# Four places instead of two for raw weight chunks in a fused four-layer kernel

## The chip, the cores and the metric

One core of one Trainium2 chip runs the whole program. Its engines are named as in the profile: PE does matrix products (PEld is its weight load), DVE, ACT and POOL work element by element, and the queue of SP (SPq in the profile) issues nearly all DMAs. The metric is the device time of one launch in microseconds. Of the kernel before, three runs were timed: 2829.66, 2829.91 and 2830.13 us, median 2829.91 us.

## What is computed

The input `x` has 16 batches of 256 positions by 256 features. Four layers are applied, each added to its own input:

- Layer 0: a gated running average along the positions, with 16 decays of its own, their blend, two gates, a product and a layer norm.
- Layer 1: per batch a softmax over masked scores, and the average that it weights.
- Layer 2: eight experts and a shared one, each `silu(h Wg) * (h Wu)` and then `Wd`, with 1024 hidden features. All nine are applied to every batch and summed with weights of the batch. In the kernel they are nine experts, so the weights of layer 2 are read as 9 x 8 = 72 chunks of 128 hidden features.
- Layer 3: `gelu(h W1 + b1)`, then `W2` for 192 of the features and one of eight small matrices, chosen by batch, for the other 64.

```
x = x + _L0_cond_ref(x, ...)
x = x + _L1_cond_ref(x, L1_cond_W1, L1_cond_b1, L1_cond_v, itok_B_0_2)
x = x + _L2_cond_ref(x, fside_Bx8_0, condB_sharedgateprob[:, None], ...)
x = x + _L3_cond_ref(x, itok_B_0_7, ...)
```

## The kernel before

**Numbers in two parts.** Every matrix product of layers 2 and 3, and those of layers 0 and 1 from batch 1 on, is made of three passes (`mm3`, L101 to L103). Each operand is split into a rounded high part (`rnd`, L88, on ACT) and the rest (`low`, L95, on DVE or POOL), and high x high, high x low and low x high are added up.

**Side work and unit work.** Layers 0 and 1 of a batch are two generators, `traces(b)` (21 steps) and `pooled(b)` (10 steps); here they are called side work. Batch 0 has versions of its own, `first_traces` and `first_pooled`. The last step of `pooled(b)` adds the result to `acc` (L460) and calls `split_x2` (the rows x<-acc), which writes the two parts of layer 2's input. Layer 2 is done by `l2_unit`, one unit for one chunk of two batches, or for two chunks of one batch: products into `pg` and `pu`, the SiLU on ACT (L742), `h` on DVE (L743), its two parts `hh` (L88 on ACT, L95 on POOL), and, two units later, the product into `y`. Each unit works on 512 columns in all.

**Order of the units.** A list called `plan` goes through positions; position p applies expert p mod 9. Batch 0 alone takes positions 0 to 4, batches 0 and 1 take 5 to 8, batch 1 alone 9 and 10. From position 11 on the next pair rides as well, so that each chunk is used by two groups; layer 3 of the first pair comes after position 13. A unit for both batches of a pair needs `pooled` of both to be done. Between units the loop calls `step()`, which advances the side work at a pace worked out from due times; in program order `pooled(1)` ends at the 16th of the 20 units of batch 0 alone. From then on what a step issues on DVE and PE is put behind the `h` and the product last issued in program order. A planner in the framework then orders each engine's instructions by priority and by its own estimate of times. Loads of chunks are given a priority 400 places ahead (`BOOST`).

**The weight chunks.** `load_chunk` brings a chunk (128 x 768 numbers, 384 KB) into a raw tile by a DMA on SP's queue (L672). ACT writes its high part and DVE or POOL its low part into a tile of the ring `w` (L88 and L95, rows w_e<-raw_e). A raw tile can be loaded anew when both have read it. The ring has ten places (`RING`); a place is free when the last product of its chunk is done. The raw tiles have two places (the pool `raws`). From position 11 on, both parts of a chunk are also written out to memory (`keep`, L696), and from position 20 on chunks come from there, without raw tiles (L665). So 160 chunks go through raw tiles: 88 of positions 0 to 10 and 72 of positions 11 to 19. In positions 0 to 4, POOL makes the low part of every third chunk or so, and DVE the others.

**The tiles of the pairs' inputs.** Layer 2's and layer 3's inputs of a pair (`x2`, `x3`) lie in the pool `xs`, which has three places of 128 x 2048 numbers. At the start one of them holds small weights (`raw_a`, in the profile small_a). The inputs of pairs 0 and 1 take two of them (first written at 59.9 and 339.7 us), and the next tile wanted is that of the first pair's layer 3, first written at 523.9 us.

Of the kernel before, what the change touches and what calls it, by code (L numbers as in the profile page):

```python
# [8 lines left out]
F32 = mybir.dt.float32  # L9
# [9 lines left out]
P = 128  # L19
# [6 lines left out]
SLACK = 16  # L26
L0_BUFS = {"bt": 3, "tr": 3, "mod": 2, "hA": 2, "hB": 2}
SECOND = 11
APART = 5
LAG = 2  # L30
BOOST = 400
# [13 lines left out]
def fused_kernel(  # L45
# [27 lines left out]
    raws = ctx.enter_context(tc.tile_pool(name="raws", bufs=2))  # L73
    xs = ctx.enter_context(tc.tile_pool(name="xs", bufs=3))
# [11 lines left out]
    def rnd(e, out_, in_):  # L86
        if e == "a":
            last_of["ca"] = A.activation(out_, in_, AF.Copy)  # L88
        elif e == "v":
            V.tensor_copy(out_, in_)  # L90
        else:
            G.tensor_scalar(out_, in_, 1.0, 1.0, ALU.mult, ALU.mult)

    def low(e, out_, in_, h):
        i = (V if e == "v" else G).tensor_tensor(out_, in_, h.bitcast(F32), ALU.subtract)  # L95
        if e == "v":
            last_of["cv"] = i
        return i
# [557 lines left out]

    kept = {}

    def load_chunk(key):
        kind = key[0]  # L660
        again = (kind, key[2])
        if kind != "c" and again in kept:
            t = ring.tile([P, 2, 768], F32R, tag="w", name="w_" + "_".join(map(str, key[:2])) + f"_{key[-1]}")
            n = 768 if kind == "e" else 384
            nc.sync.dma_start(t.bitcast(F32)[:, :, :n], kept[again])  # L665
            ring_tiles[key] = t
            return
        raw = raws.tile([P, 768], F32, tag="raw", name="raw_" + "_".join(map(str, key)))
        t = ring.tile([P, 2, 768], F32R, tag="w", name="w_" + "_".join(map(str, key[:2])) + f"_{key[-1]}")
        if kind == "e":  # L670
            n = 768
            nc.sync.dma_start(raw, wexp[key[2]])  # L672
        elif kind == "f":
            n = 384
            nc.sync.dma_start(raw[:, :n], w3[key[2]])
        else:
            n = 512
            b, i = key[1], key[2]
            nc.sync.dma_start(
                raw[:, :520],  # L680
                comb[bass.ds(eregs[b], 1), i].rearrange("o p c -> (o p) c"),
            )
            if i == 0:
                V.tensor_copy(bias3[:, b : b + 1], raw[:, 512:513])
        rnd("a", t[:, 0, :n], raw[:, :n])
        e = "v"
        if kind == "e" and key[1] == 0:

            e = "g" if key[2] < 2 else "v" if key[2] < 6 else "gv"[key[2] % 2]
        elif kind == "e" and key[1] < ALONE and key[2] % 3 == 0:  # L690
            e = "g"
        low(e, t[:, 1, :n], raw[:, :n], t[:, 0, :n])
        ring_tiles[key] = t
        if kind == "e" and key[1] >= SECOND or kind == "f":
            d = keep.tile([P, 2, n], F32, name="keep_" + "_".join(map(str, again)))
            nc.sync.dma_start(d, t.bitcast(F32)[:, :, :n])  # L696
            kept[again] = d
# [145 lines left out]
    for k in range(1, NB // 2):  # L843
        p0 = SECOND + NX * ((k - 1) // 2) + (0 if k % 2 else APART)
        rides.append((p0, p0 + NX, (2 * k, 2 * k + 1)))
# [4 lines left out]
    for pos in range(max(r[1] for r in rides)):  # L850
        e = pos % NX
# [24 lines left out]
    def prefetch(n, boost=BOOST):  # L876
        while n > 0 and nxt[0] < len(order):
            k = order[nxt[0]]
            if k[0] == "c" and k[1] not in eregs:
                eregs[k[1]] = nc.sync.value_load(eix[0:1, k[1] : k[1] + 1], min_val=0, max_val=NE - 1)  # L880
            with tc.high_priority(offset=boost) if boost else nullcontext():
                load_chunk(k)
            nxt[0] += 1
            n -= 1
# [102 lines left out]
    for i, item in enumerate(plan):  # L987
        kind, args, _, done = item[:4]
# [130 lines left out]
```

## Time and profile before

| what | value |
|---|---|
| median of three runs | 2829.91 us |
| the profiled execution, its time | 2829.02 us |
| its span, first to last instruction | 2827.0 us |
| mean granted clock of PE | 0.996 |
| PE, DVE, ACT, POOL busy | 2774.3, 1454.9, 1248.6, 1299.3 us |
| loads of expert chunks into raw tiles | 160, of 384 KB, 11.7 to 859.0 us, median 3.7 us to landing |
| read and written by DMA | 310.91 MB read, 64.21 MB written |

Times of views are microseconds from the start of the span. A line of the waits reads "who waited, for whom: total us, times, longest us". A line of the windows reads "stretch, its length, then for PE, PEld, DVE, ACT and POOL busy us and instructions, then PE's granted clock, the busy share of the DMA engines, and GB/s". A line of a tile's view reads "line, engine, operation, out<-in, count: shortest/median/longest ns, first and last start".

### The profile page before, as it was taken

How to read it: one execution, taken by the hardware profiler on the slowest of the kernel's cores; microseconds unless marked ns; L12 is line 12 of the kernel's file. 1: busy time of each engine (PE TensorE's matmuls, PEld its weight loads, DVE VectorE, ACT ScalarE, POOL GpSimd, SP SyncE). 2: the span in 40 equal slices, each digit the busy share in tenths (PEclk: the TensorE clock that was granted, in tenths of full speed). 3: DMA queues.
4: the chain of work that ended last, by engine and by line, in shares of the span. 5: the costliest groups of instructions: out<-in, count | busy, mean ns of one | idle time of the engine just before them, and what ended most of it. 6: DMA issues, size and time to landing. Idle time of an engine off the chain costs nothing.

```text
span 2827.0 us, 36929 instructions
## 1 busy us (share of the span) xinstructions
PE 2774.3 (98%) x13604; PEld 2331.4 (82%) x13604; DVE 1454.9 (51%) x2662; ACT 1248.6 (44%) x2062; POOL 1299.3 (46%) x986
## 2 busy tenths in 40 slices
PE   7889999999999999999999999999999999999999
PEld 4877898888888888888888888888888888888888
DVE  6988877865666363544545444444444542222222
ACT  5565565465444533435334443344433453233334
POOL 5755645544545353544534444444444443333333
PEclk9999999999999999999999999999999999999999
DMA  4453376396443533324433153331533242222453
GB/s 118 138 153 118 104 242 214 121 309 207 151 150 123 177 114 105 120 81 135 153 107 106 41 179 112 108 120 62 177 101 112 92 162 98 90 90 89 167 177 118
DMA packets 116998, 377.53 MB, mean 134 GB/s; under 512 B 12898, under 2 KB 31186, under 8 KB 116818
## 3 DMA queue, kind: packets, MB, share of 16 engines
q1 hardware_dynamic: 116386, 375.11, 40.1%
q8 instruction: 108, 1.77, 0.3%
q14 instruction: 72, 0.59, 0.1%
q10 hardware_dynamic: 432, 0.06, 0.0%
HBM read 310.91 MB, written 64.21 MB: 133 GB/s over the span
## 4 chain that ended last, share of the span: by engine, by line
PE 82%; DVE 7%; DMA 4%; ACT 3%; issue 2%; POOL 1%; SPq 0%; DVEq 0%; ACTq 0%; POOLq 0%
PE pg L102 8%; PE pg L103 8%; PE pg L101 8%; PE pu L103 8%; PE pu L102 8%; PE pu L101 8%; PE y L103 8%; PE y L102 8%; PE y L101 8%; DMA raw_e<-in_wexp_dram 4%; DVE w_e L95 2%; DVE tr L331 1%; ACT w_e L88 1%; PE z L101 1%; PE z L103 1%
## 5 line engine op out<-in xcount | busy, mean ns | idle before, releaser
L95 POOL TENSOR_TENSOR hh<-h,hh 128x512 fp32r<-128x512 f32 x640 | 847.7, 1325 | 1318.8 <-ACT hh L88 1298.2
L743 DVE TENSOR_TENSOR h<-h,pu 128x512 f32<-128x512 f32 x576 | 393.9, 684 | 907.4 <-PE pu L103 805.6
L88 ACT ACTIVATE hh<-h 128x512 fp32r<-128x512 f32 x640 | 403.5, 631 | 933.8 <-DVE h L743 911.6
L101 PE MATMUL pg<-x,w_e 128*128 128x512 f32 (+1 forms) x1232 | 466.0, 378 | 10.2 <-DVE h L743 6.4
L742 ACT ACTIVATE h<-pg 128x512 f32<-128x512 f32 x576 | 343.1, 596 | 299.1 <-PE pg L103 236.5
L101 PE MATMUL pu<-x,w_e 128*128 128x512 f32 (+1 forms) x1232 | 465.3, 378 | 6.9 <-ACT h L742 6.7
L103 PE MATMUL pg<-x,w_e 128*128 128x512 f32 (+1 forms) x1232 | 464.6, 377 | 1.5 <-DVE w_e L95 1.2
L102 PE MATMUL pg<-x,w_e 128*128 128x512 f32 (+1 forms) x1232 | 464.4, 377 | 1.1 <-POOL x L95 1.1
L102 PE MATMUL y<-hh,w_e 128*128 128x512 f32 (+1 forms) x1232 | 462.8, 376 | 2.2 <-POOL hh L95 2.2
L102 PE MATMUL pu<-x,w_e 128*128 128x512 f32 (+1 forms) x1232 | 463.5, 376 | 0.0
L103 PE MATMUL pu<-x,w_e 128*128 128x512 f32 (+1 forms) x1232 | 463.4, 376 | 0.0
L103 PE MATMUL y<-hh,w_e 128*128 128x512 f32 (+1 forms) x1232 | 462.7, 376 | 0.0
L101 PE MATMUL y<-hh,w_e 128*128 128x512 f32 (+1 forms) x1232 | 416.2, 377 | 2.8 <-ACT hh L88 1.6
L335 POOL TENSOR_TENSOR ta<-ta,tr 128x512 f32<-128x512 f32 x225 | 310.5, 1380 | 87.3 <-DVE tr L331 77.1
L331 DVE TENSOR_TENSOR_SCAN tr<-decay,bt 128x256 f32<-128x256 f32 x450 | 285.6, 671 | 0.0
L101 PEld LDWEIGHTS pg<-x,w_e 128*128 128x128 f32 x1232 | 232.3, 189 | 54.1 <-DVE h L743 8.9
L101 PEld LDWEIGHTS pu<-x,w_e 128*128 128x128 f32 x1232 | 232.5, 189 | 50.4 <-ACT h L742 9.5
L101 PEld LDWEIGHTS y<-hh,w_e 128*128 128x128 f32 x1232 | 231.5, 189 | 46.8 <-ACT hh L88 2.6
L102 PEld LDWEIGHTS y<-hh,w_e 128*128 128x128 f32 x1232 | 232.4, 189 | 44.6 <-POOL hh L95 2.9
L103 PEld LDWEIGHTS pg<-x,w_e 128*128 128x128 f32 x1232 | 232.4, 189 | 44.4 <-DVE w_e L95 2.0
L103 PEld LDWEIGHTS pu<-x,w_e 128*128 128x128 f32 x1232 | 232.5, 189 | 41.9
L103 PEld LDWEIGHTS y<-hh,w_e 128*128 128x128 f32 x1232 | 232.3, 189 | 41.8
(279 smaller groups left out, 3263.2 us busy)
## 6 DMA issues: line engine op xcount, KB each, us to landing
w_e<-keep_e SPq DMA_DIRECT2D x216, 768.0 KB, 4.2
raw_e<-in_wexp_dram SPq DMA_DIRECT2D x160, 384.0 KB, 3.7
keep_e<-w_e SPq DMA_DIRECT2D x72, 768.0 KB, 4.3
mod<-mdd SPq DMA_DIRECT2D x120, 256.0 KB, 3.6
w_f<-keep_f SPq DMA_DIRECT2D x56, 384.0 KB, 3.5
raw_c<-in_comb_dram SPq DMA_DIRECT2D x32, 260.0 KB, 2.7
xr<-in_xT_dram SPq DMA_DIRECT2D x16, 256.0 KB, 3.5
xt<-in_x_dram SPq DMA_DIRECT2D x16, 256.0 KB, 2.6
```

The source lines that it names most:

```text
L88: last_of["ca"] = A.activation(out_, in_, AF.Copy)
L95: i = (V if e == "v" else G).tensor_tensor(out_, in_, h.bitcast(F32), ALU.subtract)
L101: PE.matmul(o, wh, xh, start=start, stop=False, **kw)
L102: PE.matmul(o, wh, xl, start=False, stop=False, **kw)
L103: last_of["pe"] = PE.matmul(o, wl, xh, start=False, stop=stop, **kw)
L331: V.tensor_tensor_scan(tr[:, c], decay[:, d : d + 1].to_broadcast([P, S]), bt[:, c], 0.0, ALU.mult, ALU.add)
L335: G.tensor_tensor(tacc, tacc, tr, ALU.add)
L742: A.activation(h, ps_g, AF.Silu)
L743: last_of["h"] = V.tensor_tensor(h, h, ps_u, ALU.mult)
```

## The change

One more tile, `spare`, is taken from the pool `xs`, so that it is the second of its three places; it is a whole tile of 2048 numbers per partition, of which two stretches of 768 are used, at 0 and at 1024. Chunks are counted as they are loaded, and of every four, two go to the pool `raws` as before and two into the halves of `spare`, as long as they are chunks of positions 0 to 11 (96 chunks). All other chunks go to `raws`, whose two places remain. Nothing else is changed: not the ring, not the loads or their sizes, not the order in which the program asks for them.

```
+SPARE = 12
...
+    spare = xs.tile([P, 2048], F32, tag="x2", name="spare")
+    n_raw = [0]
+
+    def raw_place(key):
+        n_raw[0] += 1
+        if key[0] == "e" and key[1] < SPARE and n_raw[0] % 4 > 1:
+            o = (n_raw[0] % 4 - 2) * 1024
+            return spare[:, o : o + 768]
+        return raws.tile([P, 768], F32, tag="raw", name="raw_" + "_".join(map(str, key)))
...
-        raw = raws.tile([P, 768], F32, tag="raw", name="raw_" + "_".join(map(str, key)))
+        raw = raw_place(key)
```

## The prediction

> **What bounds the kernel now.** I read the page first: PE is busy for nearly the whole span, and its idle time lies in the first eighth.
>
> ```profile
> PE 2774.3 (98%) x13604; PEld 2331.4 (82%) x13604; DVE 1454.9 (51%) x2662; ACT 1248.6 (44%) x2062; POOL 1299.3 (46%) x986
> ...
> PE   7889999999999999999999999999999999999999
> ```
>
> PE idles for 2827.0 - 2774.3 = 52.7 us. Whatever the change does, it can't win more than that, apart from clock. The second view is a table by stretches, cut where batch 0's units begin (60), where both batches' units begin (188.4), and at 345 and 408, about where chunks of the later positions begin.
>
> ```profile
> 0.00:60.00 60.00, 44.71 (x124) 23.07 (x124) 43.00 (x104) 33.45 (x72) 35.31 (x36) 0.89 0.42 117
> ...
> 60.00:80.00 20.00, 19.85 (x162) 19.39 (x162) 15.19 (x28) 12.83 (x20) 9.98 (x7) 1.00 0.41 133
> 80.00:120.00 40.00, 32.27 (x243) 29.63 (x242) 38.03 (x68) 18.08 (x27) 34.30 (x23) 1.00 0.46 142
> 120.00:188.40 68.40, 58.48 (x443) 56.33 (x443) 49.61 (x79) 44.55 (x73) 37.97 (x26) 0.95 0.49 148
> 188.40:345.00 156.60, 148.31 (x690) 120.46 (x691) 139.71 (x230) 85.67 (x140) 95.97 (x66) 0.99 0.39 117
> 345.00:408.00 63.00, 61.69 (x491) 59.77 (x490) 47.74 (x79) 38.95 (x66) 23.19 (x17) 1.00 0.67 222
> ```
>
> The reader is to see 15.3 us of idle PE before 60, 7.7 between 80 and 120, 9.9 between 120 and 188.4, 8.3 up to 345, 1.3 up to 408. Third, the waits from 60 to 188.4, of the engines and of SP's queue:
>
> ```profile
> ACT w_e L88 <- DMA raw_e<-in_wexp_dram: 32.5, 25, 4.3
> POOL w_e L95 <- ACT w_e L88: 23.9, 6, 10.1
> ...
> DVE w_e L95 <- ACT w_e L88: 14.1, 11, 3.4
> ```
>
> ```profile
> SPq L672 <- DVE w_e L95: 37.9, 22, 3.3
> SPq L672 <- POOL w_e L95: 26.7, 10, 5.1
> ```
>
> This is a ring of waits: the load waits for a raw place, which DVE or POOL frees; ACT waits for the load; DVE and POOL wait for ACT. Fourth, the raw tile from 120 to 188.4:
>
> ```profile
> L88 ACT ACTIVATE w_e<-raw_e x22: 827/846/849, 119.7 to 185.7; 128x768 fp32r<-128x768 f32 x22
> ...
> L95 DVE TENSOR_TENSOR w_e<-raw_e,w_e x15: 930/959/1685, 120.6 to 186.3; 128x768 fp32r<-128x768 f32 x15
> L95 POOL TENSOR_TENSOR w_e<-raw_e,w_e x7: 1813/1849/2307, 119.1 to 174.6; 128x768 fp32r<-128x768 f32 x7
> ...
> DMA to landing us min/median/max: 2.8/3.1/5.1
> ```
>
> One turn of a place is 3.1 + 0.85 + 0.96 = 4.9 us, or 5.8 with POOL's 1.85. Two places give a chunk every 2.5 to 2.9 us at best. Measured, the load of chunk 24 was issued at 121.7 and that of chunk 38 at 168.7, so 3.36 us a chunk. PE needs 18 matmuls at 0.12 us from start to start (the timeline), 2.16 us, plus what side work it has.
>
> Is PE held by this? I numbered loads, roundings, low parts and each chunk's first `pg` matmul in order of start, and took the time from the end of the low part to that matmul. Chunks 0 to 9 are ready 8 to 18 us ahead: a stock. Chunks 13 to 39 (80 to 180 us) lie between -3.6 and +1.2 us: no stock. (Below zero means that the high part was used while the low one was made.) Chunks 40 to 80 are ready 6 to 34 us ahead again, chunks 81 to 90 2.6 to 6. Chunks 91 to 95 are late again (-2.6 to +2.9), but there PE idles 1.3 us in all. So raw places cost PE time from 80 to 180 us and hardly elsewhere among the 96 chunks that the change reaches.
>
> **The change part by part.** *Instructions:* none added or removed. The loads, 0.33 us each on SP, and the 0.85, 0.96 and 1.85 us of the two parts stay. *What goes:* the wait of a load for its place. With four places a turn of 4.9 to 5.8 us gives a chunk every 1.2 to 1.5 us, less than PE's 2.16. What is late next is a place in the ring. A unit's `y` comes two units after it, so of ten places six are in use and four, two units' worth (4.3 us of PE at the least), lie ahead; one load's remaining 0.85 + 0.96 or 1.85 us fits in that. SP's queue: the loads of `mod` (L322), queued behind a waiting chunk load, can only come sooner. *DMA:* landing took 3.1 us at a busy share of 0.49. At shares near 0.95, between 580 and 660, it took 4 to 6; even 5.5 gives 7.3 / 4 = 1.8 us a chunk. *The tile:* nothing waits for it. The third place of its pool is next written at 523.9, and chunk 95's low part ended at 406.7. That cover is 117 us; without it layer 3 of the first pair would wait.
>
> Now the sum, stretch by stretch.
>
> - Before 60: 0. The idle time is the chain of batch 0, and the chunks are already early.
> - 60 to 80: 0, there is stock.
> - 80 to 120: DVE is busy 38.0 of 40, mostly with scans and `bt` of `traces`. Where DVE is full, earlier loads win nothing: between 0 and 2.0. I take 1.0.
> - 120 to 188.4: PE 58.5 busy. The bounds are 0 and 9.9 idle, and the clock beside it. In the next stretch, where chunks lie ready, PE still idles 8.3 of 156.6, 5.3%. At that share 58.5 would take 61.8 us, a gain of 6.6. The clock was 0.69 and 0.88 in the eight us from 120 and 0.81 and 0.76 in those from 160, in each case after idle PE; weighted by busy time this cost 2.8 us, and if the idle time goes, 55.7 / 0.947 = 58.8, a gain of 9.6. I take 7, near the lower.
> - 188.4 to 408: 0 (bounds -2 and +2 for the planner's new order).
>
> Sum 1 + 7 = 8 us. On the clock: the Trainium skill (TensorE: Matmul & The Clock Gate, "HAM oscillation — how this bites in real kernels") says that the clock falls after gaps over about 3.4 us. Here it fell to 0.81 around a longest single gap of 2.5 us, so the trace is stricter; by the page no clock would return, and the stretch would give 6.6.
>
> The order of the instructions is the planner's and will shift everywhere after 60. Past 408 PE idles for only 52.7 - 42.7 = 10 us in 2419, so a shift there can cost or win little; I allow 3 us either way.
>
> **Rivals.** The wait that ended last at 188.4 was not a chunk: chunk 40 was ready at 178.8, but batch 1's input was written at 183.9 (ACT) and to 188.4 (POOL), and PE idled 2.05 us for DVE's `acc`. So the gain needs `pooled(1)` to come sooner too. For it speak three places where that chain stood in a queue behind a chunk: its reciprocal (163.80) behind a low part whose chunk was late, 2.9 us after the sums:
>
> ```profile
> 160.76 0.16 DVE L433 TENSOR_TENSOR sums<-sums,cntb 128x2 f32<-128x2 f32 x1 [0.28 <-ACT sc L429]
> 162.92 0.96 DVE L95 TENSOR_TENSOR w_e<-raw_e,w_e 128x768 fp32r<-128x768 f32 x1 [2.00 <-ACT w_e L88]
> 163.80 0.16 DVE L434 RECIPROCAL sums<-sums 128x2 f32<-128x2 f32 x1
> ```
>
> then `q` behind a rounding that waited 2.5 us for its load, and `pp`, whose input was ready at 171.0 and which came at 178.2 behind chunks 38 and 39. Together 2.9 + 2.5 + 7.2 = 12.6 us, more than I count on.
>
> *Rival 1, the cover is used up:* DVE (87.6 of 108.4 us from 80 on) and the chain hold the pace, and the wait for raw tiles becomes one for the ring or for DVE. Gain 0 to 4, middle 2: 2828. The full DVE before 120 speaks for it; 120 to 188.4, with DVE at 73%, against.
> The Trainium skill (SBUF — State Buffer, "Who interferes with whom") says that a DVE instruction with two SBUF inputs and a reading POOL instruction exclude each other. Low parts of 0.93 to 1.69 us agree; from 80 to 120, POOL's 34.3 with seven low parts at 0.96 make 41 of 40, no gain there, which would lower the sum by 1.
>
> *Rival 2, slower:* chunk work goes ahead of the chain. Loads have priority, so with four raw places up to two more chunks can stand before each of the ten steps of `pooled(1)`. One more low part (0.96) at each is 9.6 us; batch 1's input comes at 198, PE has run out of batch 0's units, and the time is 2829.9 + 9.6, about 2839. It decides as soon as the chain slips at all, as it is last by 5 us already. Against it: over the stretch the chunks are as many as before, and the ring holds them back.
>
> *Rival 3, not four places:* if the program's waits were set for `spare` as a whole and not for its halves, a load into one half would wait for the readers of the other, leaving about three places: 4.9 to 5.8 / 3, or 1.6 to 1.9 us, a gain of some 4 us: 2826. Against it: `ph` read small_a's first columns at 6.0 us, while its last columns' load was issued at 6.3, so waits are set for parts of a tile.
>
> **How the numbers follow.** 2829.91 - 8 = 2822 (the profiled execution: 2829.02 - 8 = 2821, span 2819). Chances: forecast 0.55, its own range 2815 to 2826; rival 1 0.25; rival 2 0.12; rival 3 0.08. The range, 2814 to 2831, goes from all bounds at their best (2 + 9.6 + 2 + 2) to just past no change and leaves out most of rival 2. 0.2% is 5.7 us, about what a measurement can tell from no change. The forecast passes it nine times in ten, rivals 1 and 3 one time in five, by the 3 us of the planner's order: faster 0.56. Slower by that: rival 2 alone, 0.11. Within: 0.33.
>
> **What would show it.** Right: between 80 and 180 ACT's 32.5 us of waiting for raw loads fall under 10, SP's waits at L672 too, chunks 13 to 39 are ready 3 us or more ahead, both batches' units begin near 180 instead of 188, the clock from 120 on is over 0.97, and everything after is shifted by the same 8 us. Rival 1: the waits are gone but the start at 188 stays, with PE waiting for `acc`, DVE or the ring (ACT for `y`). Rival 2: that start is past 192. Rival 3: loads into one half of the spare tile wait for low parts of the other. I am wrong altogether if the early part wins and the planner's new order loses it after 408.

## The result and the profile after

The changed kernel takes 2825.51 us (median of 22 runs, 2823.26 to 2827.66) beside 2829.59 us for the kernel before (22 runs, 2827.59 to 2831.41). The ratio is 0.9987, with a 95% interval of 0.9981 to 0.9992: 4.1 us less, about half of the forecast 8. The interval sets it clear of no change, but it is under the bound of 0.2%. The profiled execution took 2826.21 us with a span of 2823.9, 3.1 less than before; its mean clock is 0.994.

PE's row of the page, and its row by slices of the span, hardly move:

```profile
PE 2772.7 (98%) x13604; PEld 2332.3 (83%) x13604; DVE 1461.7 (52%) x2662; ACT 1246.8 (44%) x2061; POOL 1303.3 (46%) x986
...
PE   7889999999999999999999999999999999999999
```

**The feed changed as intended.** Some of the waits of the engines from 60 to 188.4 in the changed kernel (its lines are numbered one higher up to the loads):

```profile
POOL w_e L96 <- ACT w_e L89: 17.0, 6, 10.2
...
ACT w_e L89 <- PE y L104: 8.2, 5, 2.1
...
PE pg L102 <- DVE h L756: 7.1, 3, 3.3
...
DVE w_e L96 <- ACT w_e L89: 4.7, 7, 1.5
...
ACT w_e L89 <- DMA spare<-in_wexp_dram: 3.1, 3, 1.7
ACT w_e L89 <- DMA raw_e<-in_wexp_dram: 2.8, 2, 2.6
```

ACT's 32.5 us of waiting for loads are 5.9. In their place ACT waits 8.2 us for `y`, that is for a place in the ring: the chunks have caught up with it. Counted as in the prediction, chunks 10 to 39 are ready 0.5 to 7 us ahead of their first product (one, chunk 19, 1.5 us late), where chunks 13 to 39 lay between -3.6 and +1.2. What PE waits for longest is now `h`, which DVE makes. SP's queue in the same stretch:

```profile
SPq L685 <- DVE w_e L96: 55.5, 27, 4.2
...
SPq L685 <- POOL w_e L96: 7.5, 4, 2.6
```

These sum to 63.0, before to 64.6: the loads wait as long as they did, only each stands further ahead of its use. A queue's wait by itself says nothing of how late its transfers are.

**The time did not follow.** The stretches of the prediction, in the changed kernel (in each line PE's busy time is the first number behind the length):

```profile
60.00:80.00 20.00, 19.89 (x163) 19.64 (x164) 17.78 (x30) 13.40 (x21) 11.00 (x7) 1.00 0.46 143
80.00:120.00 40.00, 32.88 (x254) 31.97 (x254) 40.00 (x66) 20.41 (x30) 36.07 (x23) 0.96 0.55 163
120.00:188.40 68.40, 55.38 (x428) 53.30 (x426) 52.61 (x78) 41.53 (x70) 37.41 (x23) 0.93 0.57 172
188.40:345.00 156.60, 150.01 (x701) 122.14 (x702) 137.36 (x234) 83.52 (x137) 95.71 (x69) 0.99 0.35 101
345.00:408.00 63.00, 62.31 (x501) 61.22 (x500) 53.45 (x85) 39.98 (x67) 27.54 (x19) 1.00 0.70 244
```

DVE now is busy for all 40 us from 80 to 120. From 120 to 188.4 PE does less than before (428 matmuls instead of 443), and more after.

Equal stretches of two kernels hold different work, so I compared the same work: the end of the n-th `h` on DVE, one for each unit, counted from 0. Units 0 to 19 are of batch 0 alone; unit 20 is the first that needs batch 1.

| unit | before, us | after, us | difference |
|---|---|---|---|
| 10 | 123.4 | 123.4 | +0.1 |
| 14 | 148.0 | 141.5 | -6.5 |
| 18 | 174.2 | 162.7 | -11.5 |
| 19 | 185.6 | 166.7 | -18.8 |
| 20 | 192.6 | 197.1 | +4.5 |
| 34 | 261.3 | 257.1 | -4.1 |
| 200 | 1067.5 | 1064.1 | -3.4 |
| 575, the last | 2775.8 | 2772.6 | -3.2 |

The units of batch 0 alone lead by up to 18.8 us, and the step from unit 19 to 20 (7.0 us before, 30.3 after) eats all of it and 4.5 us more. Here is that step on PE, from its timeline in the changed kernel (idle time and its end stand in brackets):

```profile
175.87 1.17 PE L445 MATMUL ppt<-ident,sc 128*128 128x128 f32 x4 [5.58 <-DVE sc L437]
...
178.93 0.55 PE L102 MATMUL pg<-x,wh 128*128 128x256 f32 x1 [1.90 <-DVE q L96]
...
184.85 0.39 PE L457 MATMUL pp<-q,v 128*128 128x256 f32 x1 [1.02 <-ACT gp L305]
...
189.30 0.39 PE L102 MATMUL pso<-x,wh 128*128 128x256 f32 x1 [2.75 <-DVE acc L461]
```

Those are 11.3 us of idle PE, and no load is among their ends. `ppt` and `pp` are steps of `pooled(1)`; `pg` and `pso` are steps of batch 2's `traces`, which take turns with them: both generators write to one place in PSUM (the memory that PE's products go to), and there `pg` waits until `q` is made from `ppt`, `pp` until ACT has read `pg`, and `pso` until `acc` has taken up `pp`. Batch 1's input was written (x<-acc on ACT) at 183.9 us before and at 189.3 after, 5.4 us later. This point, where both batches are needed, is called the gate below.

A third measure serves the experiments: PE's lost time. For each matmul I took the time from its start to the next one's, less a short spacing of its shape in the same trace, at or under which a fifth of them lie (0.226 us for 512 columns, 0.117 for 256, 0.029 for the transposes). It holds idle time and a slower clock alike, and these spacings add up to 2699.9 us in both kernels.

| lost, us | 60-120 | 120-160 | 160-200 | 200-345 | 345-408 | sum | whole span |
|---|---|---|---|---|---|---|---|
| before | 13.2 | 6.1 | 10.7 | 15.1 | 4.6 | 49.6 | 117.3 |
| after | 11.4 | 3.5 | 18.5 | 11.2 | 3.1 | 47.7 | 114.1 |

Won 4.4 us up to 160, lost 7.8 at the gate, won 5.4 from there to 408. The last term is the surprise of the other sign: by 200 us the low parts of 46 chunks had been made before, of 50 after, and from 200 to 345 PE's waits for `h` of DVE fell from 4.7 to 1.7 us. As I read it, while PE stood at the gate DVE split chunks that it would otherwise have split later, when it was nearly full; no run tests this by itself.

### The profile page after: what moved, and what is told of

Read it like the earlier page. It is cut to its first block, busy times and chain, and to the rows that moved or that the text cites. A ratio compares the mean times of both kernels' runs of the same rounds, so it can differ in the third digit from the quotient of the medians.

```text
span 2823.9 us, 36967 instructions
## 1 busy us (share of the span) xinstructions
PE 2772.7 (98%) x13604; PEld 2332.3 (83%) x13604; DVE 1461.7 (52%) x2662; ACT 1246.8 (44%) x2061; POOL 1303.3 (46%) x986
## 4 chain that ended last, share of the span: by engine, by line
PE 86%; DVE 6%; DMA 2%; ACT 2%; issue 2%; POOL 1%; SPq 0%; DVEq 0%; ACTq 0%; POOLq 0%
PE pg L102 9%; PE pg L103 9%; PE pg L104 9%; PE pu L102 8%; PE pu L103 8%; PE pu L104 8%; PE y L103 8%; PE y L104 8%; PE y L102 8%; DVE w_e L96 1%; DMA raw_e<-in_wexp_dram 1%; DVE tr L332 1%; PE z L102 1%; PE z L104 1%; PE z L103 1%
```

## The experiments

Three theories stood against each other. By the first, raw places are still the limit somewhere, and the gain lies in some positions. By the second, the gate is the limit: what makes batch 1's chain (from its `t<-ta` on ACT to its input) earlier is won. By the third, two limits lie behind the raw places, DVE's work up to 408 us and the chain, and what is won against one is paid to the other. The expectations use other names: theories A and D are forms of the second theory (A: chunks of positions 5 and 6 stand before the chain; D: the chain itself is long), theory B is the part of the third that is about DVE's work, and rival C says that raw places never mattered. Edits are on top of the changed kernel unless said otherwise. Ratios are to the kernel before, with 95% intervals; the changed kernel's is 0.9987.

**Where do the four places count?** First only in positions 0 to 4:

```
-SPARE = 12
+SPARE = 5
```

> Four places for the chunks of positions 0 to 4 only; from position 5 on two. Theory A (gate): in the changed kernel batch 0's units ran 11 us ahead by 163 us, and then PE waited at the first unit of both batches for batch 1's input, written at 189.3 instead of 183.9 us, because the rounding and low parts of chunks 40 to 49 (positions 5 and 6), free of the wait for a raw place, stand before that chain on ACT and DVE. With two places for these chunks the input comes 2 to 5 us sooner than 189.3, and the time is 2822 to 2826 us. Theory B (engine totals): DVE and POOL are full over the whole stretch and the order matters little: the input stays within 1 us of 189 and the time within 1.5 us of the changed kernel's 2825.5. If the gain was made by stock in positions 5 to 11, the time is back at 2828 to 2830.

2834.79 us, 1.0019 [1.0010, 1.0028]: every expected time is missed, and it is slower than either kernel. Batch 1's input came at 194.9, 5.6 us later than in the changed kernel. Of this 3.4 us arise at one place: PE's `pg` waits 5.26 us for `q` instead of 1.90. The cause is in ACT's timeline of this kernel:

```profile
178.81 0.38 ACT L89 ACTIVATE q<-ppt 128x256 fp32r<-128x256 f32 x1 [2.51 <-PE ppt L445]
181.72 0.84 ACT L89 ACTIVATE w_e<-raw_e 128x768 fp32r<-128x768 f32 x1 [2.52 <-DMA raw_e<-in_wexp_dram]
182.46 0.36 ACT L89 ACTIVATE q<-ppt 128x256 fp32r<-128x256 f32 x1
```

The second half of `q` stands behind a rounding that waits 2.52 us for its load. In the changed kernel the halves start at 177.07 and 177.94; that is 2.8 of the 3.4 us, and a chunk's low part on DVE, ahead of the second half's, is the rest. So a chunk that is late does hold the chain, as the prediction read it from the kernel before. The other way round, four places only from position 5 on:

```
-        if key[0] == "e" and key[1] < SPARE and n_raw[0] % 4 > 1:
+        if key[0] == "e" and ALONE <= key[1] < SPARE and n_raw[0] % 4 > 1:
```

> Four places for the chunks of positions 5 to 11 only; positions 0 to 4 keep two. Theory A: the feed of batch 0's units is as slow as before, chunk 39 is late as before, batch 1's input comes at 183 to 187 us, and little is gained: 2827.5 to 2830 us. Theory B: the gain of 4 us comes from DVE's work on chunks moved out of 188 to 408 us, which these places allow as well: 2825 to 2827.

2830.69 us, 1.0007 [0.9998, 1.0016]: no gain. The chain begins at 124.8, as before (124.7), and ends at 185.7, where theory A had it; the time is 0.7 us past A's range and far from B's. Neither half of the change wins anything alone; the 4.1 us need both.

**Can the gate be opened sooner?** Due times of `pooled(1)` set earlier in program order, in the changed kernel and (second) in the kernel before:

```
-    due = [(at[boards[b]] - SLACK, ready[b]) for b in range(1, NB, 2)]
+    due = [(at[boards[b]] - (2 * SLACK if b == 1 else SLACK), ready[b]) for b in range(1, NB, 2)]
```

> The changed kernel, with batch 1's side work due 32 instead of 16 units of cost ahead of its first use (four of batch 0's units sooner in program order). Theory A: the gate opens sooner, batch 1's input is written before 181 us, PE's idle time between 160 and 195 falls from 13 to under 6 us, and the time is 2816 to 2822 us. Theory B: DVE is full, the side work only pushes the chunks back; the input comes no sooner than 187 us, and the time is 2824 to 2828.

> The kernel before, two raw places, with the same earlier due time of batch 1's side work. Theory A: chunk 39 still comes at about 176 us, so the feed is the gate and at most 3 us are won: 2827 to 2829.5 us. Rival C (the side work's pace alone was the limit, raw places never mattered): the same gain as with four places and the earlier due time, 2816 to 2822.

2832.81 us, 1.0015 [1.0006, 1.0024], and 2834.16 us, 1.0018 [1.0009, 1.0027]. The input comes at 189.1 and 185.5 (189.3 and 183.9 without the edit). All expected times are missed: asked for sooner in program order, the chain ends no sooner.

Next, fewer steps of batch 2's `traces` among those of `pooled(1)`. The two generators share one PSUM place (tag "ps" of `ps_l`), so each step of the one waits for the other's:

```
-            front = FRONT if b else FRONT0
+            front = (1 if b == 1 else FRONT) if b else FRONT0
```

> The changed kernel, but only one step of batch 2's traces instead of four is mixed with batch 1's pooled steps; the other three come after them. So the tiles ph, pm and pg of batch 2 no longer pass through the one place of the PSUM tile that batch 1's chain needs for pt, po, ptr, pa, psc, ppt and pp. Theory D (the chain from the end of batch 1's traces to its input, 59 to 66 us in every run so far, is the gate, and it is long because it shares that place with batch 2's ph, pm and pg: 3.7, 3.5 and 6 us between the neighbours in the changed kernel): the input comes 9 to 14 us sooner than 189.3, PE's gaps between 165 and 192 fall from 12 to under 5 us, and the time is 2815 to 2821 us. Theory B (DVE is full, the order matters little): the deferred steps are paid for in the next stretch, and the time stays within 2 us of 2825.5 although the input comes sooner. If the chain does not get shorter, the place was not what holds it, and the input stays at 187 to 190.

> The kernel before, two raw places, with the same three steps of batch 2 taken out of batch 1's chain. Theory D with the feed as second gate: the input comes at 170 to 176, but batch 0's units end at about 180 to 182 us as before because chunk 39 is ready no sooner than 176, so at most 4 us are won against the kernel before: 2825 to 2829. Rival C (only the chain matters, raw places never did): as much as with four places, 2815 to 2821.

2837.88 us, 1.0031 [1.0019, 1.0043], and on the kernel before 2836.39 us, 1.0028 [1.0019, 1.0038]. The second shows most. Its chain takes 47.4 us instead of 59.2, the input comes at 172.3, 11.6 us sooner, and the gate is open. In the changed kernel the same edit shortens the chain by 3.4 us only, to 57.5. Both times are longer than any expected. The stretches of two_front1 around and after the gate, and those of the kernel before:

```profile
160.00:200.00 40.00, 36.74 (x242) 33.11 (x241) 24.38 (x40) 24.93 (x39) 13.61 (x9) 1.00 0.47 149
200.00:345.00 145.00, 131.74 (x596) 106.26 (x594) 131.34 (x224) 77.77 (x123) 95.30 (x64) 0.98 0.39 117
```

```profile
160.00:200.00 40.00, 33.08 (x212) 29.60 (x211) 30.77 (x56) 23.27 (x37) 20.94 (x14) 0.96 0.52 159
200.00:345.00 145.00, 136.76 (x637) 110.97 (x636) 128.34 (x212) 78.84 (x130) 87.58 (x61) 0.99 0.38 116
```

30 matmuls more up to 200, 41 fewer up to 345, where the deferred steps are made up. The second theory falls: an open gate alone is paid for in the next stretch, and more than that (batch 3's input came at 412.0 instead of 403.9). Here it is not DVE that PE waits for longer: from 200 to 345 its waits for `h` of DVE are 4.9 us (before 4.7), those for the SiLU on ACT 5.4 (before 1.7), and those for low parts on POOL 2.6 (before none).

**Is it the priority of the chunks?** Chunks of positions 5 to 8, then those of 0 to 4, without their 400 places:

```
-            with tc.high_priority(offset=boost) if boost else nullcontext():
+            up = 0 if k[0] == "e" and ALONE <= k[1] < NX else boost
+            with tc.high_priority(offset=up) if up else nullcontext():
```

(in the second the condition is `k[1] < ALONE`)

> The changed kernel, with the loads, roundings and low parts of the chunks of positions 5 to 8 in program order instead of 400 places ahead. If chunks 40 to 49 standing before the chain on DVE and ACT make it late, the input comes 2 to 5 us sooner than 189.3 (the reciprocal waited 2.2 us behind two low parts), and the time is 2821 to 2825. Theory D: they cost the chain at most 2 us, the input comes at 187 to 190, and the time is 2824 to 2828.

> The changed kernel, with the chunks of positions 0 to 4 in program order instead of 400 places ahead. With four places batch 1's traces ended 3.7 to 4.7 us later than with two (t rounded at 128.4 to 129.4 instead of 124.7 to 124.9), with DVE busy for 40.0 of 40 us from 80 to 120. If that is because low parts of chunks go ahead of the scans on a full DVE, t comes back to 124 to 126 and the input with it, to 185 to 187; batch 0's units lose part of their 11 us lead, and the time is 2822 to 2826. If the lateness has another cause, t stays at 128 or later, and the time is 2825 to 2830.

2826.82 us and 2826.29 us, both 0.9992 [0.9983, 1.0001], not to be told from the changed kernel. Each time lies in one of its expected ranges, but the inputs, at 191.8 and 187.6, lie outside those named for them. With the first edit the input is later; with the second `t` comes at 127.0 instead of 128.4, but the time stays. So the priority is at most a small part of what makes the chain late.

**More work ahead of the gate.** With batch 0 alone in six (seven) positions, units 20 to 23 (27) no longer need batch 1; six also on the kernel before:

```
-ALONE = 5
+ALONE = 6
...
-    due = [(at[boards[b]] - SLACK, ready[b]) for b in range(1, NB, 2)]
+    due = [(at[boards[b]] - (SLACK + 16 * (ALONE - 5) if b == 1 else SLACK), ready[b]) for b in range(1, NB, 2)]
```

> The changed kernel, but batch 0 rides alone for six positions instead of five (and batch 1 for six later), with the side work of batch 1 at the same steps a unit as before. PE's work is the same in sum; four more of batch 0's units stand before the first unit that needs batch 1's input. Theory D (the feed's gain of 11 us was lost at that gate, where PE stood idle from 170 to 190): the extra units, 17 us of PE, fill the gap, PE's gaps from 160 to 215 fall from 13 to under 5 us, and the time is 2815 to 2820 us. Theory B (DVE's work to 408 us sets the sum and the gap only moves): DVE has 10 more of batch 0's chunks to split before the gate, the idle time comes back in the next stretch, and the time is 2823 to 2829.

> The kernel before, two raw places, with the same six positions alone. The feed then binds for 48 chunks instead of 40: at 3.36 us a chunk the last of them is ready at about 207 us, PE waits for chunks until then, and the gate is no longer felt. Theory D: nothing is won, 2827 to 2834. If the two places were never what cost PE time, it gains as much as with four places.

> As alone6, with seven positions. Theory D: six are enough to fill the gap of 11 us with 17 us of units, so the seventh wins nothing more: within 2 us of alone6. Theory B: each further position moves DVE's splitting of chunks forward and the time gets longer than alone6's by 2 us or more.

2832.21 us, 1.0012 [1.0003, 1.0021]; 2836.55 us, 1.0027 [1.0017, 1.0038]; 2849.85 us, 1.0072 [1.0058, 1.0086]. With six, both times are past what any theory allowed; with seven, the further loss is what theory B expected. The changed kernel with six:

```profile
160.00:200.00 40.00, 34.12 (x282) 33.58 (x281) 32.49 (x53) 28.49 (x49) 15.66 (x11) 0.96 0.66 200
200.00:345.00 145.00, 132.16 (x642) 109.59 (x643) 130.17 (x223) 78.40 (x122) 88.78 (x63) 0.95 0.34 101
```

The gate's lost time falls from 18.5 to 7.8 us, and that of 200 to 345 rises from 11.2 to 23.5; with seven, 29.0 us are lost at the next pair's gate (345 to 408). The cover is only moved. Between the two kernels with six, four places are again worth 4.3 us.

**Less work for DVE.** Last, in positions 0 to 8 the low parts that DVE makes become a second rounding on ACT. The true low parts of these weights are left out, so its time is no version's; it shows what DVE's share costs:

```
-        low(e, t[:, 1, :n], raw[:, :n], t[:, 0, :n])
+        if kind == "e" and key[1] < NX and e == "v":
+            rnd("a", t[:, 1, :n], raw[:, :n])
+        else:
+            low(e, t[:, 1, :n], raw[:, :n], t[:, 0, :n])
```

> The changed kernel with DVE relieved: for the chunks of positions 0 to 8 whose low part DVE makes (some 60 of 72, 0.96 us each), ACT writes the rounded chunk a second time in its place (0.85 us each). So the low parts of those weights are left out and the high ones counted twice; PE, POOL and the loads do the same work. Theory B (a full DVE holds the whole stretch from 80 to 345 us): DVE is busy for under 37 of 40 us from 80 to 120, t is rounded before 126, batch 1's input comes before 184, PE's gaps from 200 to 345 halve, and the time is 2803 to 2817. Theory D (the chain from t to the input, 60 us in nearly every run, is what holds, whatever DVE has to do): t may come 2 to 4 us sooner, but the input comes 59 to 62 us after it, the gaps from 200 to 345 stay, and the time is 2819 to 2826.

2813.64 us, 0.9945 [0.9932, 0.9959]: 11.9 us under the changed kernel, as theory B expected. 58 instructions move (DVE has 2604 instead of 2662, ACT 2119 instead of 2061). Its stretches:

```profile
80.00:120.00 40.00, 38.41 (x316) 37.80 (x315) 31.12 (x61) 31.70 (x47) 36.62 (x27) 1.00 0.61 192
160.00:200.00 40.00, 25.75 (x123) 21.56 (x122) 22.56 (x52) 21.00 (x35) 12.53 (x10) 0.79 0.35 106
200.00:345.00 145.00, 144.80 (x733) 122.65 (x732) 107.75 (x201) 96.40 (x156) 83.35 (x64) 1.00 0.37 110
```

PE is nearly full from 80 to 120 and from 200 to 345, where DVE is no longer. At the gate little changed, against B and about as D had it: the chain begins 5.2 us sooner (`t` at 123.2), but takes 62.4 us, the input comes at 185.7, and PE's longest waits from 160 to 195 are the same ones:

```profile
PE ppt L445 <- DVE sc L437: 5.4, 1, 5.4
PE pso L102 <- DVE acc L461: 2.8, 1, 2.8
PE pg L102 <- DVE q L96: 1.9, 1, 1.9
...
```

The lost times side by side, in us, by the labels of the expectations (two_ is an edit of the kernel before, with two places):

| kernel | 60-120 | 120-160 | 160-200 | 200-345 | 345-408 | sum | input of batch 1 at |
|---|---|---|---|---|---|---|---|
| before | 13.2 | 6.1 | 10.7 | 15.1 | 4.6 | 49.6 | 183.9 |
| after | 11.4 | 3.5 | 18.5 | 11.2 | 3.1 | 47.7 | 189.3 |
| four_0_4 | 13.5 | 2.3 | 23.9 | 11.1 | 5.3 | 56.0 | 194.9 |
| four_5_11 | 14.5 | 6.0 | 12.6 | 15.5 | 2.1 | 50.7 | 185.7 |
| side_sooner | 9.6 | 5.8 | 18.3 | 14.1 | 2.8 | 50.7 | 189.1 |
| two_side_sooner | 13.6 | 6.5 | 14.5 | 15.0 | 5.2 | 54.7 | 185.5 |
| front1 | 10.6 | 6.3 | 17.1 | 16.8 | 4.0 | 54.8 | 185.0 |
| two_front1 | 14.0 | 7.3 | 5.5 | 22.2 | 4.3 | 53.3 | 172.3 |
| no_boost_5_8 | 14.0 | 2.9 | 18.9 | 11.1 | 2.9 | 49.8 | 191.8 |
| no_boost_0_4 | 11.9 | 2.5 | 18.2 | 11.2 | 3.0 | 46.8 | 187.6 |
| alone6 | 14.8 | 2.6 | 7.8 | 23.5 | 6.8 | 55.5 | 199.8 |
| two_alone6 | 13.4 | 6.3 | 11.5 | 21.0 | 10.2 | 62.3 | 184.2 |
| alone7 | 14.9 | 2.1 | 3.6 | 24.0 | 29.0 | 73.7 | 199.4 |
| act_low | 4.8 | 3.7 | 20.9 | 2.8 | 2.9 | 35.0 | 185.7 |

Whatever the order, 47 to 62 us are lost up to 408 (74 with seven positions); only less work for DVE brings it to 35. Of the three theories the third is the one that fits all runs. act_low shows its first limit, DVE's work, directly. The second, the chain, rests on the gate that stays in act_low (20.9 us); and two_front1 adds that what is won at the gate can also be paid on ACT and POOL.

## Why the prediction was right, and twice too large

The time lies in the stated range, and most of the chances stood elsewhere: 0.56 on a gain past 0.2%, and 0.33 on what came. The sum was not met term by term. Its large term turned into a loss and a term of 0 into a gain, so that the time ended between the two is in part luck.

**That raw places hold the feed: right.** ACT's waits and the ring came as forecast, the stock nearly so (0.5 to 7 us ahead, where 3 or more was named); what was late next was a place in the ring, as named. That the loads' own waits at SP would fall was wrong (64.6 to 63.0). Rival 3, that the two halves of `spare` would wait for each other, is excluded: chunk 29's load was issued at 121.68 us, just after its own half's last low part (121.65), while the other half's ran from 125.33; chunk 37's at 142.69, after 142.66, while the other's ran from 143.13.

**60 to 120, gain 1.0: nearly right.** Lost time fell by 1.8 us, but unit 10 came no sooner (+0.1 us). DVE was the limit there, now for 40.0 us of 40: 6.2 of PE's 7.2 us of waits from 80 to 120 are for its `h`. act_low shows it from the other side (6.6 us less lost). The Trainium skill's rule of the shared port (SBUF — State Buffer, "Who interferes with whom"), by which this term was 0, agrees with the trace: in the changed kernel two low parts took 4.63 us on DVE from 62.41 to 67.04, beside two of POOL's from 61.72 to 66.24, where one alone takes 0.96.

**"120 to 188.4: ... I take 7": this step failed.** Up to 160 it won 2.6 us, at the gate it lost 7.8: together a loss of 5.2 us where a gain of 7 was forecast. The prediction had written its condition down, "the gain needs `pooled(1)` to come sooner too", and had taken the 12.6 us that the chain stood behind chunks as paying for it. The chain did win at its end: from `sums` to the input it took 23.1 us before and 16.4 after. But it began 3.7 us later (`t` at 128.4 instead of 124.7; act_low, where DVE is not full, has it at 123.2), and from `t` to `sums` it took 44.5 instead of 36.1 us. There the units went ahead of it: when its `psc` product started, 16 units had passed `h` before, at 156.4 us, and all 20 after, at 168.6. Chunks that are ready let the units of batch 0 pass, and the chain's steps wait for the same engines. From then on PE had nothing else to do. All kernels of this record agree: in the nine with four places in positions 0 to 4 this first part takes 44.5 to 47.8 us and 19 or 20 units are ahead of `psc`, in the five without 34.9 to 39.5 us and 16.

Part of the forecast's 12.6 us was not there either. `pp` stood 7.2 us in the kernel before, but not for chunks alone: batch 2's `pg` had the shared place in PSUM from 171.89 until ACT had read it at 175.90, so 4.9 of the 7.2 us were `traces`. And the reciprocal still stands behind two low parts, of chunks that now are early, as DVE's timeline of the changed kernel shows:

```profile
172.91 0.14 DVE L434 TENSOR_TENSOR sums<-sums,cntb 128x2 f32<-128x2 f32 x1
173.45 0.96 DVE L96 TENSOR_TENSOR w_e<-raw_e,w_e 128x768 fp32r<-128x768 f32 x1 [0.40 <-ACT w_e L89]
174.39 0.96 DVE L96 TENSOR_TENSOR w_e<-spare,w_e 128x768 fp32r<-128x768 f32 x1
175.26 0.16 DVE L435 RECIPROCAL sums<-sums 128x2 f32<-128x2 f32 x1
```

That is rival 2's mechanism, 2.2 us of it. Rival 1's sign, "the waits are gone but the start at 188 stays, with PE waiting for `acc`, DVE or the ring", is what the trace shows: the first product for both batches moved from 188.4 to 191.6, just short of the 192 given for rival 2.

**"188.4 to 408: 0": wrong by 5.4 us in the good direction.** More chunks were split by 200 us, and PE waited less for DVE afterwards. So the time lies between the forecast and rival 1, by a route that neither described.

**The clock: wrong.** Over 0.97 was forecast from 120 on, and 0.93 came, since the idle time was not removed but gathered in one place. Two rows around the 5.58 us gap:

```profile
172.00:176.00 4.00, 0.13 (x1) 0.14 (x1) 3.57 (x8) 2.26 (x6) 0.00 (x0) 0.60 0.73 245
176.00:180.00 4.00, 2.10 (x9) 1.65 (x10) 0.93 (x3) 0.77 (x2) 0.00 (x0) 0.50 0.85 270
```

By the Trainium skill (TensorE: Matmul & The Clock Gate, "HAM oscillation — how this bites in real kernels") a gap over about 3.4 us does this, and here it agrees (0.50 after 5.58 us). The kernel before had 0.63 from 122 to 126 with no idle time over about 1 us around it, so a gap that long is not needed. The slow clock fell on the chain itself: the 24 products of `pg` took 4.9 us (178.93 to 183.83) where they had taken 3.0 (171.89 to 174.89), so it held the chain 1.9 us longer there.

**After 408: right**: PE idles 9.5 us instead of 10.1, 0.6 of the 3 us allowed (1.0 by the lost time).

What stays open: of the chain's 60 us, two_front1 takes off about 12 on the kernel before, and front1 only 3.4 on the changed one. Whether that is the shared place in PSUM or the engines' time for the deferred steps, these runs do not separate; how much of the rest is the planner's order and how much the steps' own length was not tried. That the chain's first part is longer where the feed is faster all fourteen kernels show; that the units passing it are the cause is read from the order in the traces, and no run tested it by itself.

## What to carry to other kernels

Before pricing a wait that goes, ask which point the work behind it must meet next, and whether the other side of that point gets sooner by the same edit; if not, the wait moves there. Compare two kernels by the time of the same n-th instruction: a lead that grows to 18.8 us and is gone one unit later names the place at once. When every change of order only moves the lost time, look for an engine that is full on both sides of the gate: here 58 instructions fewer on DVE were worth 11.9 us, and no change of order on top of the changed kernel was measurably faster than it.

## What the runs showed of the hardware

In the changed kernel the granted clock fell to 0.50 and 0.62 in the eight us after the gap of 5.58 us, and to 0.73 and 0.84 from 188 to 196, after one of 2.75; there a 512-column matmul took up to 0.63 us instead of 0.39. In the changed kernel a chunk's low part on DVE took 1.3 to 2.6 us when it ran beside one on POOL, 0.96 alone. A rounding on ACT that waits for its load held a finished operand's rounding behind it for 2.5 us: ACT kept to its order.
